# One decoder kernel, one edit: local attention's normalising roots shared and its background work kept in program order, media attention kept in program order with its routing spread wider

## The chip, the core and the metric

The kernel runs on one core of a Trainium2 chip. The metric is device time in microseconds (us), the median of three runs. Durations and waits below come from one profiled execution, whose own time stands in the table further down.

## What is computed

Two layers of a pre-norm decoder over x of shape 8 x 512 x 256 (float32). Cut to what matters here:

```python
x = x + self_attention(layernorm(x))
x = x + cross_attention(layernorm(x), ctx, ctx, adj, mask)     # 16 heads of 16
x = x + local_transformer(layernorm(x))                        # two layers l = 0, 1 of:
    #   h = shift_token(x); q, k, v = split(h @ wqkv[l])       # 8 heads of 64
    #   q, k = l2norm(q) * qs, l2norm(k) * ks; q, k = rotary_xpos(q, k)
    #   o = windowed softmax(q k^T) v                          # window 128, own and previous block
    #   x = x + o @ wo[l];  x = x + gated_gelu_ffn(norm(shift_token(x)))
x = x + quantized_attention(layernorm(x))
x = x + media_attention(layernorm(x), ctx, key_mask)           # 8 heads of 64
x = x + switch_moe(layernorm(x))                               # 8 experts, capacity 512, top 1
```

The edit touches the two local attentions, the media attention and the part of the mixture of experts (the routing) that runs beside the media attention.

## The kernel before

The 4096 rows lie in SBUF as `self.x`, 32 tiles of 128 rows; one batch row b is four of them. Stages follow one another in `fast_stages`, and each stage prepares the first batch row of the next one while it finishes (`Ahead.step`). The order on an engine is not the order of the Python code: the framework's list scheduler places an instruction when its inputs and buffers look ready to it, lower-numbered work first. Two tools of the code overrule it. `high_priority(AT_ONCE)` lets a block go ahead of whatever else is ready. `issue_after(ins)` puts what the block traces on the engine of `ins` behind `ins` in that engine's queue; it is an order only, not a wait. `together` (line 1461) uses both to keep the 4, 8 or 16 matmuls of one score or weighting group adjacent. In the cross attention, `paced` holds prepared vector work behind the softmax multiplies of the iteration before the last one.

`local_attention` (line 1832 on) is used for both layers. Its main loop goes over pairs of steps. A step pair computes the scores of one of four head pairs c of one batch row (`scores`: 8 matmul tiles, then the mask added by VectorE at L2003, then the exponential by ScalarE at L2007), then the weighted values of the head pair before (`weigh`, L2014 and L2031) and, for every second c, the row sums. These form the backbone. Between them the loop issues background work, a few small closures ("thunks") at a time:

- `prepare(b + 1)`: transposes of the rows (`turn`, L1869), twelve projections (`project(b, i, j)` for row tile i and j = q, k, v, L1885), the rotary step (`rotate`) and the transposes of q and k by heads (`turn_heads`, L1928, evacuated by ScalarE at L1931). A q or k projection leaves PSUM twice on ScalarE: as its square (L1892) and as a copy (L1893). A v projection leaves on VectorE (L1890). `rotate` runs wholly on VectorE as soon as both q and k of one row tile exist: sum of squares (L1901), a 128x16 reciprocal root by Newton steps (L1905, L1473 to L1477: eleven small instructions), and five passes over q and k (L1908 to L1919).
- `later`, a heap of delayed thunks (`Background`). Its clock advances by one per `tick`. The softmax sums go to DRAM and back (`inverted`), are multiplied in on GpSimd (`times_rows`), and the output projection `project_out` follows (L2057), whose result VectorE adds to the rows at L2062. The four projections of a batch row are entered 4 ticks after the division.

Projections, transposes and output projections share two PSUM banks named `pj`; in the cross attention there is one. So whoever evacuates a `pj` bank decides when TensorE may write it again.

`stage_media_attention` (line 2813 on) is built alike: `scores` and `weigh` are the backbone, `prepare(b + 1)` and `later` the background, two ticks' worth of thunks at most per step. After the last output projection of a batch row, `route(b)` enters the routing: statistics, normalisation (L157), two transposes (L3065), the router matmuls (L3074), choice of the expert, counting (L3105, L3106), placement, and four indirect DMAs from GpSimd (L3137) that send the rows to their slots.

Of the kernel before, what the change touches and what calls it, by code (L numbers as in the profile page):

```python
# [1277 lines left out]
class FastDecoder(Decoder):  # L1278
# [553 lines left out]
    def local_attention(self, l, y, ahead):  # L1832
# [45 lines left out]
        def project(b, i, j):  # L1878
            d = held[b]
            if j == 0:  # L1880
                d["qk"] = self.alloc(first, [P, 2 * S], F32, "la_qk", bufs=3)
                d["sq"] = self.alloc(first, [P, 2 * S], F32, "la_sq")
# [6 lines left out]
            if j == 2:  # L1889
                nc.vector.tensor_copy(d["v"][:, i, :], ps)  # L1890
# [6 lines left out]
        def rotate(d, i):  # L1897
            qk = d["qk"]
            ss = self.alloc(first, [P, 16], F32, "la_ss")
            rn = self.alloc(first, [P, 16], F32, "la_rn")  # L1900
# [11 lines left out]
            r = self.alloc(first, [P, 2 * S], F32, "la_r")  # L1912
# [7 lines left out]
            d["rows", i] = qk  # L1920
# [15 lines left out]
        def prepare(b):  # L1936

            def P_(i, j):
                return lambda: project(b, i, j)

            def T_(i):
                return lambda: turn_heads(b, i)
# [20 lines left out]
        with self.tc.tile_pool(  # L1963
# [21 lines left out]
            def scores(n):  # L1985
# [33 lines left out]
            def weigh(n):  # L2019
# [24 lines left out]
                def divide(rows):  # L2044
# [9 lines left out]
            def project_out(b, i):  # L2054
# [7 lines left out]
                nc.vector.tensor_tensor(yt, yt, ps[:, :C], ALU.add)  # L2062
# [3 lines left out]
            for pair in range(0, n + 2, 2):  # L2066
# [751 lines left out]
    def stage_media_attention(self, w, out):  # L2818
# [5 lines left out]
        with self.tc.tile_pool(reuse_waits="tile", name="ma", bufs=2) as pool, self.tc.tile_pool(  # L2824
# [153 lines left out]
            for pair in range(0, n + 2, 2):  # L2978
# [37 lines left out]
    def routing(self, pool, psum, later, out):  # L3016
# [18 lines left out]
        def route(b):  # L3035
# [483 lines left out]
```

## Time and profile before

| | us |
|---|---|
| median of 3 runs (lowest, highest) | 3094.61 (3087.45, 3096.63) |
| the profiled execution | 3094.66 |
| its span, first to last instruction | 3092.7 |
| TensorE busy in the span | 2842.4 (92%) |
| VectorE / ScalarE / GpSimd busy | 2158.3 / 1155.1 / 409.6 |
| mean granted TensorE clock | 0.974 |

The stages lie one after another in the span: cross attention up to about 662 us, with the start of local attention 0 woven into its end; local attention 0 to about 1120; its feed-forward part to about 1400; local attention 1 to about 1810; its feed-forward part to about 2080; quantized attention to about 2390; media attention to about 2840; experts to the end. Cut into such stretches, TensorE is busy as follows (each row of the table is from a table of stretches of 80 us; the columns are busy us of 80).

| stretch (us) | TensorE | VectorE | ScalarE | granted clock |
|---|---|---|---|---|
| 480 to 560, cross attention | 76.36 | 76.09 | 59.62 | 1.00 |
| 560 to 640, cross into local attention | 62.90 | 74.25 | 47.74 | 0.94 |
| 640 to 720, cross into local attention | 59.62 | 57.13 | 27.13 | 0.94 |
| 880 to 960, local attention 0 | 74.19 | 66.49 | 30.57 | 0.98 |
| 1520 to 1600, local attention 1 | 74.64 | 65.92 | 31.93 | 1.00 |
| 2560 to 2640, media attention | 77.56 | 52.80 | 30.49 | 1.00 |

"Busy" is the time in which an engine had an instruction in work, and "granted clock" is the share of full speed that TensorE was allowed. In the list of waits each line names an instruction group, what released it, the sum of the idle time before it in us, how often, and the longest.

### The profile page before, as it was taken

The page shows a single profiled execution, that of the slowest core. Times are in us where ns is not written, and L with a number is a line of the kernel's source. Part 1 is how long each engine was busy: PE and PEld are TensorE (multiplying, and loading weights), DVE is VectorE, ACT ScalarE, POOL GpSimd, SP SyncE. Part 2 cuts the span into 40 slices and gives each one's busy share as a digit, 9 for nine tenths or more (in the row PEclk, how much of TensorE's full clock was granted, in tenths as well). Part 3 has the DMA queues.
Part 4 walks back from the last instruction along what each step waited for, and adds up shares of the span by engine and source line. Part 5 has one row for each costly group of instructions (what it writes and reads, how often), then busy time and mean ns, then how long its engine had stood idle before and what let it go on. Part 6 is the DMA issues. An engine that isn't in the chain of part 4 may idle for free. (4 is left out here: it accounts for less than half of the span.)

```text
span 3092.7 us, 40203 instructions
## 1 busy us (share of the span) xinstructions
PE 2842.4 (92%) x14929; PEld 1507.6 (49%) x14944; DVE 2158.3 (70%) x4962; ACT 1155.1 (37%) x1623; POOL 409.6 (13%) x389
## 2 busy tenths in 40 slices
PE   8999999969999999999999999999786999997998
PEld 5653333225555556555555556555344334434665
DVE  7458999977887894357887898548788766665110
ACT  2237777724334321124344331115263443441111
POOL 1111111100001010000101111112111123231111
PEclk9999999989999999999999999999997999998999
DMA  7011212101001001001000012010332122223231
GB/s 242 1 35 50 71 49 70 36 19 56 15 15 29 15 24 36 0 1 43 22 15 22 22 38 69 14 41 28 125 122 76 52 93 83 90 69 96 98 139 61
DMA packets 130696, 168.74 MB, mean 55 GB/s; under 512 B 51760, under 2 KB 79665, under 8 KB 128442
## 3 DMA queue, kind: packets, MB, share of 16 engines
q1 hardware_dynamic: 126394, 154.48, 16.0%
q0 software_dynamic: 4096, 11.59, 1.0%
q8 instruction: 119, 1.95, 0.3%
q14 instruction: 87, 0.71, 0.1%
HBM read 113.12 MB, written 47.50 MB: 52 GB/s over the span
## 5 line engine op out<-in xcount | busy, mean ns | idle before, releaser
L1885 PE MATMUL pj<-w,la_hT 128*128 128x512 f32 x720 | 342.8, 615 | 32.7 <-DVE x L2062 16.3
L1732 DVE TENSOR_TENSOR x_e<-x_e,x_share 128x1024 f32<-128x1024 f32 x256 | 317.6, 1283 | 16.7 <-ACT x_e L1731 16.5
L1731 ACT ACTIVATE x_e<-sc 128x1024 f32<-128x1024 f32 x256 | 249.4, 1023 | 82.0 <-PE sc L1720 82.0
L1885 PEld LDWEIGHTS pj<-w,la_hT 128*128 128x128 f32 x720 | 131.7, 194 | 189.3 <-issue 118.1
L2007 ACT ACTIVATE la_e<-la_e 128x1024 f32<-128x1024 f32 (+1 forms) x128 | 121.1, 952 | 209.2 <-DVE la_e L2003 209.2
L2890 ACT ACTIVATE ma_e<-sc,ma_bias 128x1024 f32<-128x1024 f32 x128 | 135.8, 1110 | 165.3 <-PE sc L2884 165.3
L2216 ACT ACTIVATE lf_gate<-pj,lf_b 128x512 f32<-128x512 f32 (+1 forms) x82 | 56.3, 687 | 346.6 <-PE pj L2195 337.2
L2897 DVE TENSOR_TENSOR ma_esum<-ma_esum,ma_e 128x1024 f32<-128x1024 f32 x96 | 129.8, 1353 | 71.3 <-ACT ma_e L2890 34.8
L2195 PE MATMUL pj<-lf_hnT,w 128*128 128x512 f32 (+1 forms) x368 | 171.7, 595 | 0.6 <-DVE lf_hid L2221 0.6
L2003 DVE TENSOR_TENSOR la_e<-sc,la_mask 128x1024 f32<-128x1024 f32 (+1 forms) x128 | 137.0, 1081 | 41.1 <-PE sc L1995 41.0
L3262 POOL TENSOR_TENSOR la_oT<-la_o,x_wide 128x512 f32<-128x512 f32 x64 | 88.3, 1387 | 571.0 <-DMA x_wide<-invs 315.4
L1748 PE MATMUL po<-x_e,x_v 128*32 128x512 f32 x1024 | 138.1, 612 | 21.9 <-DVE x_e L1732 15.2
L2195 PE MATMUL sc<-lf_hnT,w 128*128 128x512 f32 x336 | 157.9, 592 | 0.0
L1720 PE MATMUL sc<-x_q,x_k 32*128 32x512 f32 x1024 | 151.3, 640 | 1.7 <-DVE sa_ok L1448 1.4
L2267 PE MATMUL po<-w,lf_hid 128*128 128x256 f32 x640 | 148.8, 379 | 0.0
L2221 DVE SCALAR_TENSOR_TENSOR lf_hid<-sc,lf_b,lf_gate 128x512 f32<-128x512 f32 x70 | 52.4, 748 | 126.9 <-PE sc L2195 126.9
L1995 PE MATMUL sc<-la_qkT 64*128 64x256 f32 (+1 forms) x1024 | 124.2, 373 | 12.3 <-ACT la_qkT L1931 11.3
L1892 ACT ACTIVATE la_sq<-pj 128x512 f32<-128x512 f32 x120 | 71.4, 595 | 170.3 <-PE pj L1885 170.3
L2057 PE MATMUL pj<-w,la_oT 128*128 128x256 f32 x512 | 122.3, 385 | 11.3 <-DVE x L2062 9.4
L2884 PE MATMUL sc<-ma_qT,ma_kT 64*128 64x512 f32 x512 | 129.9, 626 | 0.0
L2267 PEld LDWEIGHTS po<-w,lf_hid 128*128 128x128 f32 x640 | 117.8, 190 | 20.2 <-issue 6.7
L2908 PE MATMUL po<-ma_e,ma_v 128*64 128x512 f32 x512 | 124.2, 606 | 0.0
(493 smaller groups left out, 5296.2 us busy)
## 6 DMA issues: line engine op xcount, KB each, us to landing
x_wide<-invs SPq DMA_DIRECT2D x184, 128.0 KB
w<-in_f_w_dram SPq DMA_DIRECT2D x16, 1024.0 KB
kv<-kv_o SPq DMA_DIRECT2D x56, 256.0 KB
slots<-x_empty SPq DMA_DIRECT2D x8, 1028.0 KB
x_mask<-in_x_maskT_dram SPq DMA_DIRECT2D x8, 1024.0 KB
ma_kT<-kv SPq DMA_DIRECT2D x8, 1024.0 KB
ma_v<-kv SPq DMA_DIRECT2D x8, 1024.0 KB
ex_rows<-slots SPq DMA_DIRECT2D x7, 1028.0 KB
```

The costliest lines, as they stand in the source:

```text
L1720: nc.tensor.matmul(pair[r // 2][:, r % 2, :], d["k"][rows, g, kt * P : (kt + 1) * P], d["q"][rows, e, g, :], start=True, stop=True,)
L1731: nc.scalar.activation(ex, d["e"][rest][p], AF.Exp)
L1732: nc.vector.tensor_tensor(ex, ex, d["share"][:, kt, :].unsqueeze(1).broadcast_to([P, 2, 512]), ALU.mult)
L1748: nc.tensor.matmul(d["po"][32 * r : 32 * r + 32, :], d["v"][:, kt, 8 * g + 2 * r + e, :], ex[r // 2][:, r % 2, :], start=(kt == 0), stop=( ...
L1885: nc.tensor.matmul(ps, d["hT"][:, k, i * P : (i + 1) * P], wqkv[:, k, j * S : (j + 1) * S], start=(k == 0), stop=(k == 1),)
L1995: nc.tensor.matmul(both[half][:, r, jj * 256 : jj * 256 + to - j * P], d["qkT"][rows, 4 + c, j * P : (j + 1) * P], d["qkT"][rows, c, j * P ...
L2003: nc.vector.tensor_tensor(ex[:, :, :n_cols], ps[:, :, :n_cols], mask[:, :n_cols].unsqueeze(1).broadcast_to([P, 2, n_cols]), ALU.add,)
L2195: nc.tensor.matmul(ps[:m, :], w1[:, k, at : at + m], held[b]["hnT"][:, k, :], start=(k == 0), stop=(k == 1))
L2267: nc.tensor.matmul(ps[:, :C], held[b]["hid"][:, f, i * P : (i + 1) * P], w2[:, f, :], start=(f == 0), stop=False,)
L2884: nc.tensor.matmul(both[m // 2][:, r, :], d["k"][rows, c, kt * P : (kt + 1) * P], d["q"][rows, c, :], start=True, stop=True,)
L2890: nc.scalar.activation(ex, ps, AF.Exp, bias=bias[:, b * NST + kt : b * NST + kt + 1], scale=0.125)
L2897: nc.vector.tensor_tensor(d["sum", c], d["sum", c], ex, ALU.add)
```

## The change

In local attention:

- `in_turn()` is new. It queues the TensorE instructions of its block behind the newest TensorE instruction traced so far. Every background thunk and every tick of the main loop now runs inside it, and the stepping of the next stage at the end of the loop too. Backbone instructions are not bound by it.
- `rotate` is cut into `square` (the sum of squares of one row tile), `root` (one reciprocal root for two row tiles, 128x32) and `rotate` (the five passes). `prepare` lists them in a new order: two q/k tiles are projected, squared and rooted before the first is rotated, and all v projections come last, each beside a `turn_heads`. The number of thunks is 18 before and after.
- The v projection leaves PSUM on ScalarE and no longer on VectorE.
- `la_qk` has 4 buffers where it had 3; `la_r` has 1 where it had 2.
- The mask addition and the addition of the output projection get the priority `AT_ONCE` on VectorE.
- The output projections are entered 9, 12, 15 and 18 ticks after the division, where all four were entered at 4.

In media attention, background thunks and ticks run inside `in_turn()`; and for batch rows 0 to 5 the routing's delays grow by 2 ticks up to the choice of the expert and by 4 from the counting on.

```diff
+    def in_turn(self):
+        return self.tc.issue_after(self.newest(mybir.EngineType.PE))
...
             if j == 0:
-                d["qk"] = self.alloc(first, [P, 2 * S], F32, "la_qk", bufs=3)
+                d["rows", i] = self.alloc(first, [P, 2 * S], F32, "la_qk", bufs=4)
...
             if j == 2:
-                nc.vector.tensor_copy(d["v"][:, i, :], ps)
+                nc.scalar.copy(d["v"][:, i, :], ps)
             else:
                 nc.scalar.activation(d["sq"][:, j * S : (j + 1) * S], ps, AF.Square)
-                nc.scalar.copy(d["qk"][:, j * S : (j + 1) * S], ps)
+                nc.scalar.copy(d["rows", i][:, j * S : (j + 1) * S], ps)
             if j == 1:
-                rotate(d, i)
+                d["sq", i] = d["sq"]
+
+        def square(b, i):
+            d = held[b]
+            if i % 2 == 0:
+                d["ss"] = self.alloc(first, [P, 2, 16], F32, "la_ss")
             nc.vector.tensor_reduce(
-                ss, d["sq"].rearrange("p (h d) -> p h d", d=64), AX.X, ALU.add
+                d["ss"][:, i % 2, :], d["sq", i].rearrange("p (h d) -> p h d", d=64), AX.X, ALU.add
             )
+        def root(b):
+            d = held[b]
+            d["rn"] = self.alloc(first, [P, 2, 16], F32, "la_rn")
+            ss, rn = (x.rearrange("p i h -> p (i h)") for x in (d["ss"], d["rn"]))
             nc.vector.tensor_scalar(ss, ss, 1e-24, None, ALU.max)
             self.rsqrt(first, rn, ss, "la_rt")
+        def rotate(b, i):
+            d = held[b]
+            qk, rn = d["rows", i], d["rn"][:, i % 2, :]
...
-            r = self.alloc(first, [P, 2 * S], F32, "la_r")
+            r = self.alloc(first, [P, 2 * S], F32, "la_r", bufs=1)
...
             return [
-                [lambda: turn(b, 0), lambda: turn(b, 1), P_(0, 0)],
-                [P_(0, 1), P_(1, 0)],
-                [P_(1, 1), P_(0, 2)],
-                [P_(2, 0), T_(0)],
-                [P_(2, 1), P_(1, 2)],
-                [P_(3, 0), P_(3, 1), T_(1)],
-                [P_(2, 2), T_(2)],
-                [P_(3, 2), T_(3)],
+                [one((turn, 0)), one((turn, 1)), one((p, 0, 0)), one((p, 0, 1), (s, 0))],
+                [one((p, 1, 0)), one((p, 1, 1), (s, 1), (root,))],
+                [one((p, 2, 0), (r, 0)), one((p, 2, 1))],
+                [one((p, 3, 0), (r, 1)), one((p, 3, 1))],
+                [one((p, 0, 2), (s, 2)), one((t, 0), (s, 3), (root,))],
+                [one((p, 1, 2), (r, 2)), one((t, 1))],
+                [one((p, 2, 2), (r, 3)), one((t, 2))],
+                [one((p, 3, 2)), one((t, 3))],
             ]
...
-                    nc.vector.tensor_tensor(
-                        ex[:, :, :n_cols], ps[:, :, :n_cols],
-                        mask[:, :n_cols].unsqueeze(1).broadcast_to([P, 2, n_cols]), ALU.add,
-                    )
+                    with self.tc.high_priority(self.AT_ONCE):
+                        nc.vector.tensor_tensor(
...
-                            later.add(4, lambda i=i: project_out(b, i))
+                            later.add(9 + 3 * i, lambda i=i: project_out(b, i))
...
-                nc.vector.tensor_tensor(yt, yt, ps[:, :C], ALU.add)
+                with self.tc.high_priority(self.AT_ONCE):
+                    nc.vector.tensor_tensor(yt, yt, ps[:, :C], ALU.add)
...
                 for i in (pair, pair + 1):
-                    later.tick(1)
+                    with self.in_turn():
+                        later.tick(1)
                     if i < n:
                         for thunk in ready[i % 8]:
-                            thunk()
-                            later.tick(1)
+                            with self.in_turn():
+                                thunk()
+                                later.tick(1)
                     if i == n - 6:
                         early.close()
                     if i > n - 6:
-                        ahead.step()
+                        with self.in_turn():
+                            ahead.step()
...
                         if thunk is not None:
-                            thunk()
-                    later.tick(2)
+                            with self.in_turn():
+                                thunk()
+                    with self.in_turn():
+                        later.tick(2)
...
+            slow = 2 if b < B - 2 else 0
             later.add(1, stats)
             later.add(2, norm)
-            later.add(3, lambda: turn(0))
-            later.add(4, lambda: turn(1))
-            later.add(5, logits)
-            later.add(6, choose)
-            later.add(8, count)
-            later.add(9, place)
+            later.add(3 + slow, lambda: turn(0))
+            later.add(4 + slow, lambda: turn(1))
+            later.add(5 + slow, logits)
+            later.add(6 + slow, choose)
+            later.add(8 + 2 * slow, count)
+            later.add(9 + 2 * slow, place)
             for i in range(NST):
-                later.add(10 + i, lambda i=i: send(i))
+                later.add(10 + 2 * slow + i, lambda i=i: send(i))
```

More of the change, by code (lines that the diff above doesn't have):

```diff
@@ L1889, in project @@
             if j == 2:
-                nc.vector.tensor_copy(d["v"][:, i, :], ps)
+                nc.scalar.copy(d["v"][:, i, :], ps)
             else:
                 nc.scalar.activation(d["sq"][:, j * S : (j + 1) * S], ps, AF.Square)
-                nc.scalar.copy(d["qk"][:, j * S : (j + 1) * S], ps)
+                nc.scalar.copy(d["rows", i][:, j * S : (j + 1) * S], ps)
             if j == 1:
-                rotate(d, i)
[L1897 to L1900, printed above, removed]
+                d["sq", i] = d["sq"]
[3 more added lines that the diff above has]
+                d["ss"] = self.alloc(first, [P, 2, 16], F32, "la_ss")
             nc.vector.tensor_reduce(
-                ss, d["sq"].rearrange("p (h d) -> p h d", d=64), AX.X, ALU.add
+                d["ss"][:, i % 2, :], d["sq", i].rearrange("p (h d) -> p h d", d=64), AX.X, ALU.add
             )
+        def root(b):
+            d = held[b]
+            d["rn"] = self.alloc(first, [P, 2, 16], F32, "la_rn")
+            ss, rn = (x.rearrange("p i h -> p (i h)") for x in (d["ss"], d["rn"]))
             nc.vector.tensor_scalar(ss, ss, 1e-24, None, ALU.max)
             self.rsqrt(first, rn, ss, "la_rt")
+        def rotate(b, i):
+            d = held[b]
+            qk, rn = d["rows", i], d["rn"][:, i % 2, :]
             q3 = qk.rearrange("p (h d) -> p h d", d=64)
@@ L1919, in rotate @@
             nc.vector.tensor_tensor(qk, qk, r, ALU.add)
-            d["rows", i] = qk
         def turn_heads(b, i):
@@ L1936, in prepare, with one, thunk @@
         def prepare(b):
[L1938 to L1942, printed above, removed]
-            return [
-                [lambda: turn(b, 0), lambda: turn(b, 1), P_(0, 0)],
-                [P_(0, 1), P_(1, 0)],
-                [P_(1, 1), P_(0, 2)],
-                [P_(2, 0), T_(0)],
-                [P_(2, 1), P_(1, 2)],
-                [P_(3, 0), P_(3, 1), T_(1)],
-                [P_(2, 2), T_(2)],
-                [P_(3, 2), T_(3)],
+            def one(*calls):
+                def thunk():
+                    for f, *args in calls:
+                        f(b, *args)
+                return thunk
+            p, t, s, r = project, turn_heads, square, rotate
+            return [
+                [one((turn, 0)), one((turn, 1)), one((p, 0, 0)), one((p, 0, 1), (s, 0))],
[6 more added lines that the diff above has]
+                [one((p, 3, 2)), one((t, 3))],
             ]
@@ L2002, in scores @@
                     ex = self.alloc(pool, [P, 2, 512], F32, "la_e", bufs=6)
-                    nc.vector.tensor_tensor(
-                        ex[:, :, :n_cols], ps[:, :, :n_cols],
-                        mask[:, :n_cols].unsqueeze(1).broadcast_to([P, 2, n_cols]), ALU.add,
-                    )
+                    with self.tc.high_priority(self.AT_ONCE):
+                        nc.vector.tensor_tensor(
+                            ex[:, :, :n_cols], ps[:, :, :n_cols],
+                            mask[:, :n_cols].unsqueeze(1).broadcast_to([P, 2, n_cols]), ALU.add,
+                        )
                     nc.scalar.activation(ex[:, :, :n_cols], ex[:, :, :n_cols], AF.Exp, scale=-1.0)
```

## The prediction

> **What bounds the kernel.** I read the page's first part, then a table of stretches, then TensorE's list of waits in each stretch, and last the timelines of the worst places. TensorE is busy for 2842.4 of 3092.7 us, and where it is the bound, only its idle time and its lost clock can be won.
>
> [...] By the rows the change has no part in that: it removes or adds no matmul[...]. So I let only the idle time count, and nothing below it.
>
> Three stretches inside the stages that are touched, from the table of stretches (columns: stretch; its length; busy us and instructions of TensorE, weight loads, VectorE, ScalarE, GpSimd; granted clock; DMA share; GB/s):
>
> ```profile
> 720.00:1110.00 390.00, 363.11 (x2177) 208.38 (x2177) 317.43 (x632) 158.26 (x256) 38.02 (x39) 0.99 0.07 20
> 1360.00:1790.00 430.00, 402.21 (x2247) 231.33 (x2246) 334.29 (x639) 171.76 (x280) 39.25 (x38) 1.00 0.07 22
> 2390.00:2800.00 410.00, 389.86 (x1668) 164.60 (x1666) 282.60 (x688) 167.42 (x188) 104.12 (x95) 0.99 0.22 73
> ```
>
> TensorE idles 27, 28 and 20 us in them, so they hold 75 us at most. The waits of TensorE in the first stretch (local attention 0; sum, times, longest):
>
> ```profile
> PE pj L1885 <- DVE x L2062: 8.2, 12, 0.9
> PE sc L1995 <- ACT la_qkT L1931: 5.7, 6, 0.9
> PE pj L2057 <- DVE x L2062: 4.7, 6, 0.8
> PE pj L1928 <- DVE la_rn L1473: 4.3, 7, 1.0
> PE pj L1928 <- DVE la_qk L1919: 1.4, 4, 0.8
> ```
>
> Half of it is a `pj` bank that waits for VectorE to add an output projection; the waits come in every batch row and none is over 1 us. Layer 1 shows the same lines with 8.1, 5.6, 4.7, 3.8 and 1.3. In media attention one line carries it:
>
> ```profile
> PE pj L3065 <- DVE mo_rows L157: 12.9, 6, 2.4
> ```
>
> The dearest place is the seam between cross attention and local attention 0, 560 to 720 us, where TensorE idles 17.1 + 20.4 = 37.5 us. Its timeline and stretches:
>
> ```profile
> 635.36 3.78 PE L1885 MATMUL pj<-w,la_hT 128*128 128x512 f32 x4 [10.13 <-DVE la_v L1890]
> 658.73 3.78 PE L1885 MATMUL pj<-w,la_hT 128*128 128x512 f32 x4 [4.18 <-DVE la_v L1890]
> 663.98 1.98 PE L1885 MATMUL pj<-w,la_hT 128*128 128x512 f32 x4
> ...
> 630.00:635.40 5.40, 0.04 (x1) 0.04 (x1) 5.13 (x11) 0.00 (x0) 0.00 (x0) 0.50 0.00 0
> 635.40:639.20 3.80, 3.80 (x8) 1.26 (x12) 3.80 (x4) 0.00 (x0) 0.00 (x0) 0.50 0.00 0
> ...
> 596.00:662.00 66.00, 47.94 (x244) 14.46 (x244) 59.99 (x100) 32.53 (x43) 3.47 (x2) 0.88 0.08 17
> ```
>
> With a single `pj` bank here, a v projection waits for a copy that stands on VectorE behind a whole rotation. But VectorE works through the stall (5.13 of 5.40), and from 596 to 662 it is busy 60 of 66 us: this seam is bound by VectorE, and freeing the bank alone does not free it.
>
> **The seam, step by step.** The change takes from VectorE, for batch row 0: four v copies (684 ns each, L1890), 2.7 us; and two of four root chains. One chain in the timeline runs from 628.78 to 631.04, 2.26 us; eleven instructions of some 0.17 us do not get twice as long for 32 columns instead of 16[...] (I allow 0.2 us), so 2 x 2.1 = 4.2. Together 6.9 us less on the bounding engine. The copies go to ScalarE (580 ns each at L1893), which is idle half of this stretch; what is queued behind them there are exponentials, up to 0.6 us later.
>
> Then the clock. [...]after 10.13 and after 4.18 us a projection took 3.78 instead of 1.98 us, so each costs 1.8 more. [...]by the rows a 2.16 us wait in media attention is followed by 4.7 us at a clock of 0.67 (1.55 lost, after one of six such gaps), and three stretches of 10 us in local attention 0 (800, 910, 1030 us) stand at 0.83, 1.7 us each, with no gap over 1 us near. [...]by the rows up to 3.6 + 1.5 + 5.1. I take 3 at the seam, 4 in the local attentions and 1 in media, since the rows decide.
>
> Seam: 6.9 + 3 = 10 us gained. Bounds: 0 (the last output projections arrive through a chain of DMAs, a wait for `x_wide` that ends only at 679.5, whatever VectorE does) and 25 (two thirds of the 37.5).
>
> **The local attentions, both layers' loops.** (a) Output projections: 12.9 + 12.8 = 25.7 us of waits. They are entered three ticks apart instead of in a burst, and their addition (0.41 us) goes ahead on VectorE; it still waits for an instruction in work, at most 1.4 us, while the other bank covers a projection. I leave 4: gain 22. (b) Transposes waiting for rotations (L1473, L1919, and L1893): 6.2 + 6.6 = 12.8. A rotation now stands two groups ahead of its `turn_heads`, some 14 us against its five passes of 5.2 (rows L1908 to L1919): gain 8. (c) Scores waiting for the last `la_qkT` copy, 5.7 + 5.6: `turn_heads(3)` is still the last thunk of a row, nothing gained. (d) The clock, 4.
>
> (e) What the order costs. A projection takes 1.78 us (18 records in 7.99 us in one unbroken run, four records each) and is evacuated in 1.17 by ScalarE, so runs of projections are safe with two banks. A `turn_heads` is not: each half is 0.55 us of TensorE and 0.58 of ScalarE copy plus some 0.1 of signalling. Walked through with two banks (v projection, half, half, v projection), 0.16 + 0.06 us stay exposed; with 56 of them in the two loops, 12 us. Before, backbone matmuls were placed between the halves and hid this. After `turn`, the first projection waits for `la_hT`, 0.43 where it shows (14 times: 6). I take 12 of these 18, since the next scores are not bound by the order and can fill some; bounds 0 and 36 (then all of (a), (b) and (d) is given back). 22 + 8 + 4 - 12 = 22 us gained.
>
> What lies beside other work: 56 v copies in the loops (14 batch rows of four) cost ScalarE 56 x 0.58 = 32 us over two stages where it is busy 158 of 390 and 172 of 430 us; VectorE loses 14 x 6.9 = 97 us over both loops, where it stood at 317 of 390, and that gives nothing directly. `la_r` with one buffer only orders VectorE against itself. `la_qk` with four covers the four tiles now held until their transposes. If the ScalarE cover were gone, each projection would wait for its bank; that is the rival below. No DMA is moved in this part.
>
> **Media attention.** Six waits, batch rows 0 to 5, are exactly those whose transposes are moved by 2 ticks (some 7 us); the chain they wait for (statistics, eleven root instructions, four normalisations) was late by 2.2 us. All 12.9 go. The program order forbids early transposes of `prepare`, which have shown one 2.0 us wait; the routing's transposes and logits now meet them in the same ticks on two banks: I charge 2. Counting, placing and the 24 indirect DMAs (1179 ns each on GpSimd's queue) move by 4 ticks; queued behind them are `ma_oT` multiplications and copies into `ma_esum`, on a GpSimd busy 104 of 410 us, and nobody reads the slots before the experts. Batch rows 6 and 7 keep their delays, so the end (11.8 us for the first expert's rows) stays. With 1 of clock: 12 gained; bounds 8 and 15.
>
> **Sum.** 10 + 22 + 12 = 44 us. The profiled execution took 3094.66 and the median is 3094.61, so they need no correction: 3050.6.
>
> **Rivals.**
> - *The order gives back what it wins in the local attentions*: (e) at its bound of 36, gain 0 there; the seam gives 8 and media 12: 3075. For it: every wait of the loops is under 1 us and small enough to be only renamed, and TensorE's order was already filled densely. Against: the largest line is removed by priority and spacing, not by order.
> - *More goes*: (a), (b) and (d) in full with the gaps of (e) filled by backbone work, 45; the seam 25, media 14: 3011. For it: VectorE falls from 81% to about 70% of the loops, so its queue shortens for everything.
> - *Slower: ScalarE's queue takes over the `pj` banks.* ScalarE now evacuates all projections and all transposes, in TensorE's strict order. If each half of a `turn_heads` meets one exponential (1.06 us) ahead of its copy, 112 halves lose 119 us, of which 12 are charged already: 3158. It decides from 44 / 112 = 0.4 us per half on. Against: two exponentials per 14 us of loop, ScalarE under half busy.
> - *It does less than it says*: the order binds background TensorE work alone; if the scheduler had it so already, seam and media come partly and the rest cancels: about 3090, within the noise, if media's waits are renamed too.
>
> **How the numbers follow.** Forecast (3030 to 3062) 0.45, given back 0.19, more 0.20, slower 0.10, no change 0.06 (it does less). Predicted time 3051. The range reaches to the two neighbours that gain, 3011 and 3075, with media and seam at their ends (sizes of both signs in (e)): 3008 to 3084. A measurement of this kernel can tell 0.3% (9 us) from no change: faster 0.84, within 0.06, slower 0.10.
>
> **What would show it.** In the new profile: the waits on the added output projection (L2062's successor) under 3 us per layer, or (a) is wrong; waits of transposes on `la_qkT` and `la_v` copies by ScalarE of about 12 us in all, or (e) is; no 10 us gap and at most one half-clock stretch in the seam, with VectorE busy there about 7 us less; no `mo_rows` wait before batch row 6; half as many root instructions (192 become 96). The prediction is wrong if TensorE's idle time over the two loops does not fall from 55 us to some 36, or if the idle time stays and busy time falls.

## The result, and the profile after

The changed kernel takes 3051.07 us (median of four runs, 3046.02 to 3056.84), the kernel before beside it 3091.31 us. The ratio is 0.9865 with a 95% interval of [0.9846, 0.9883]. By the ratio that is 41.7 us less (the medians differ by 40.2), where the sum had 44. The profiled execution took 3056.84 us, the slowest of the four, with a span of 3054.9 (before: 3092.7), so the profile shows 37.8 of it.

To see where the time came from I read in both traces when certain instructions first start (before / after, the line numbers of the new kernel are a few higher):

| first start of | before | after | stretch that ends here, change |
|---|---|---|---|
| scores of local attention 0 | 696.0 | 696.9 | seam and all ahead of it: +0.9 |
| second product of feed-forward 0 | 1159.2 | 1145.9 | local attention 0: -14.2 |
| scores of local attention 1 | 1401.6 | 1387.5 | feed-forward 0: -0.8 |
| second product of feed-forward 1 | 1855.0 | 1831.9 | local attention 1: -9.0 |
| scores of media attention | 2391.5 | 2367.0 | feed-forward 1 and quantized: -1.4 |
| first expert product | 2851.9 | 2814.0 | media attention: -13.4 |

The seam gave nothing where 10 had been forecast, the two local attentions 23.2 (22), the media attention 13.4 (12). How much such differences mean can be read from later kernels that run the same instructions in a stage. Four profiles of the same local attentions (the kernel after and three below, without one of the orders or the media part) lie at 448.9 to 450.6 us and 442.5 to 444.4. Ten profiles of the same seam put the first scores anywhere from 687.9 to 700.7 us, so for the seam one profile says little. The same stretches as before, moved to where they now lie, from the table of stretches of the kernel after (columns: stretch; its length; busy us and instructions of TensorE, weight loads, VectorE, ScalarE, GpSimd; granted clock; DMA share; GB/s):

```profile
708.00:1098.00 390.00, 367.04 (x2243) 214.95 (x2241) 293.21 (x500) 181.46 (x294) 44.23 (x40) 1.00 0.07 21
1388.00:1818.00 430.00, 403.98 (x2400) 232.90 (x2397) 322.47 (x679) 193.89 (x313) 47.97 (x43) 0.99 0.10 29
2365.00:2775.00 410.00, 399.28 (x1723) 167.52 (x1723) 294.25 (x718) 173.37 (x196) 112.17 (x98) 1.00 0.22 75
```

VectorE has less to do, ScalarE more, as the diff says. TensorE's idle time in the media stretch fell from 20 to 11 us; in the local ones it is still 23 and 26. TensorE's waits in local attention 0 of the kernel after (sum, times, longest):

```profile
PE pj L1939 <- DVE x L2076: 16.2, 16, 1.6
PE po L2027 <- ACT la_o L2044: 3.4, 2, 3.1
PE pj L1939 <- ACT la_qkT L1942: 2.8, 1, 2.8
...
PE pj L1889 <- ACT la_qkT L1942: 1.6, 1, 1.6
```

The wait on the added output projection, which was to fall to under 3 us a layer, rose from 12.9 to 16.2 (layer 1: 12.8 to 14.5). It only changed its victim: a projection or an output projection before, a transposition of the heads now. The waits on the rotation are gone but for 0.4 us, and so are those of the scores on `la_qkT`, which I had left standing. This is one such wait in the timeline, first TensorE, then VectorE (start, duration, engine, line; in brackets the idle time before it and what ended it):

```profile
831.61 1.99 PE L2070 MATMUL pj<-w,la_oT 128*128 128x256 f32 x8
833.44 1.88 PE L1889 MATMUL pj<-w,la_hT 128*128 128x512 f32 x4
836.90 0.66 PE L1939 MATMUL pj<-ident,la_qk 128*128 128x128 f32 x4 [1.58 <-DVE x L2076]
```

```profile
833.49 0.69 DVE L1928 TENSOR_TENSOR la_r<-la_qk,la_sin 128x512 f32<-128x512 f32 x1
834.10 0.68 DVE L1929 TENSOR_TENSOR la_r<-la_qk,la_sin 128x512 f32<-128x512 f32 x1
834.70 0.68 DVE L2055 COPY la_total<-sum 128x512 f32<-128x512 f32 x1
835.30 1.21 DVE L1930 TENSOR_TENSOR la_qk<-la_qk,la_cos 128x1024 f32<-128x1024 f32 x1
836.44 0.41 DVE L2076 TENSOR_TENSOR x<-x,pj 128x256 f32<-128x256 f32 x1
```

The output projection is done at 833.6. Its addition has priority, but that only chose its place when the queue was laid down; behind the instruction in work three more still stand ahead of it, and it starts 2.8 us later. A row of the table of stretches says why:

```profile
822.00:852.00 30.00, 26.68 (x165) 16.34 (x163) 29.36 (x48) 12.39 (x21) 1.77 (x1) 1.00 0.07 19
```

In these 30 us of a batch row's 56, VectorE is busy for 29.36. Over the whole row it is busy 40 of 56, and that average is what I had argued from. In the 30 us that matter there is no slack. The kernel before had such a half too (here with 28.31 us):

```profile
826.00:856.00 30.00, 27.71 (x138) 16.89 (x136) 28.31 (x50) 9.60 (x16) 2.95 (x2) 1.00 0.06 19
```

The additions do come sooner than before. Counted over the timelines of local attention 0, they start on average 1.6 us behind their projection, where it was 2.5 us. But now only a v projection of 1.9 us stands between the projection and a transposition that takes the same bank.

### The profile page after: what moved, and what is told of

Read it like the earlier page. It is cut to its first block, busy times and chain, and to the rows that moved or that the text cites. A ratio compares the mean times of both kernels' runs of the same rounds, so it can differ in the third digit from the quotient of the medians.

```text
span 3054.9 us, 39805 instructions
## 1 busy us (share of the span) xinstructions
PE 2839.3 (93%) x14929; PEld 1513.9 (50%) x14944; DVE 2063.4 (68%) x4546; ACT 1192.1 (39%) x1687; POOL 428.7 (14%) x389
## 5 line engine op out<-in xcount | busy, mean ns | idle before, releaser
L1889 PE MATMUL pj<-w,la_hT 128*128 128x512 f32 x720 | 333.3, 603 | 5.2 <-ACT la_qkT L1942 4.5
L1736 DVE TENSOR_TENSOR x_e<-x_e,x_share 128x1024 f32<-128x1024 f32 x256 | 315.8, 1276 | 14.3 <-ACT x_e L1735 14.2
L3283 POOL TENSOR_TENSOR la_oT<-la_o,x_wide 128x512 f32<-128x512 f32 x64 | 97.9, 1541 | 753.0 <-DMA x_wide<-invs 647.9
L2914 DVE TENSOR_TENSOR ma_esum<-ma_esum,ma_e 128x1024 f32<-128x1024 f32 x96 | 120.6, 1260 | 58.8 <-ACT ma_e L2907 30.0
L2027 PE MATMUL po<-la_e,la_v 128*64 128x256 f32 (+1 forms) x1024 | 125.2, 369 | 6.7 <-ACT la_o L2044 6.0
```

The source lines that it names most:

```text
L1736: nc.vector.tensor_tensor(ex, ex, d["share"][:, kt, :].unsqueeze(1).broadcast_to([P, 2, 512]), ALU.mult)
L1889: nc.tensor.matmul(ps, d["hT"][:, k, i * P : (i + 1) * P], wqkv[:, k, j * S : (j + 1) * S], start=(k == 0), stop=(k == 1),)
L2027: nc.tensor.matmul(out[:, j * P : to], lhsT(j), ex[:, jj * 256 : jj * 256 + to - j * P], start=(j == 0), stop=(j == 3), skip_group_check=True,
```

## Experiments

Two lines of thought stand against each other in them. That of the forecast: the gain comes from order, spacing and priority, and the relief of VectorE acts in the seam alone. Its rival: the order does nothing, and the gain in the local attentions comes from the VectorE work that was taken away. Each expectation puts them into numbers for its kernel. The ratios are to the kernel before on the same chip, which took 3091.3 to 3098.0 us; the kernel after stands at 0.9865.

### Is the order in the local attention worth anything?

```diff
-                    with self.in_turn():
-                        later.tick(1)
+                    later.tick(1)
```

(likewise at the other two places of the loop)

> The changed kernel without the program order in local attention (the three uses of in_turn in its loop are taken out; the new list of prepared work, the shared roots, the v copies on ScalarE, the priorities and the spacing stay). Theory A: the order itself removed the small stalls of the transposes and the scores, so taking it out brings back some 10 to 20 us (about 3062 to 3071, with 3051 for the changed kernel). Theory B: the built program issues TensorE's work of both loops in the same order with and without it, all but one transpose at the end of layer 1, so nothing moves: within 5 us of the changed kernel, ratio to before 0.985 to 0.988, and the waits of the loops the same to 2 us.

3055.8 us, 0.9859 [0.982, 0.9899], and the same waits on the added projection, 16.4 and 14.6. In the two traces TensorE's sequences differ in the place of one transposition, at the end of local attention 1, and those of VectorE and ScalarE not at all. The order binds nothing here (theory B). This run also serves as the kernel after on this chip.

### What is the media part worth?

```diff
-            slow = 2 if b < B - 2 else 0
+            slow = 0
...
-                            with self.in_turn():
-                                thunk()
+                            thunk()
```

> The changed kernel with the media attention and the routing delays of before. From the traces the stretch from the first media scores to the first expert matmul fell by 13.4 us (460.4 to 447.0). Theory: parts add up, so this one loses 12 to 14 us: about 3064, ratio to before 0.990 to 0.992, and six waits of the routing's transposes on mo_rows of some 2.1 us are back. Rival: part of the fall was a better clock by chance, then it loses 8 or less.

3065.5 us, 0.9906 [0.9875, 0.9938]; the media stretch takes 460.5 us again, as before the change (447.0 after). The wait on the routing's rows in TensorE's list of waits, first here, then in the kernel after:

```profile
PE pj L3082 <- DVE mo_rows L157: 17.3, 8, 3.9
```

```profile
PE pj L3084 <- DVE mo_rows L157: 2.0, 1, 2.0
```

That is the wait of the forecast, and its size (over the same stretch the kernel before has 17.1 us, with the waits of the last two batch rows). Later I took away the order alone and kept the delays:

```diff
-                    with self.in_turn():
-                        later.tick(2)
+                    later.tick(2)
```

> The kernel after, with the wider routing delays of the media attention but without its issue in program order. Theory A (the order in the media attention carries part of the 13.4 us that the media stretch gave): the stretch from the first media scores to the first expert product goes from 447.0 us back to some 453, and the whole to some 3057. Theory B (the order does nothing, because TensorE's instructions were already issued in nearly that order; the wider delays carry all of it): the stretch stays at 447 to 450 us and the whole at 3051 to 3056 (0.986 to 0.987 of before).

0.9867 [0.9843, 0.9891], and a media stretch of 449.9 us. The wider delays carry the media part. The order adds 3 us at most, and more likely nothing: the kernel without the order in local attention, which keeps the media order, has 449.6 us as well. Over all kernels with the wider delays the stretch is 447.0 to 450.7 us, so they are worth 10 to 13 us.

### Is it VectorE's work?

Each of the two reliefs was undone alone. First the v copies:

```diff
-                nc.scalar.copy(d["v"][:, i, :], ps)
+                nc.vector.tensor_copy(d["v"][:, i, :], ps)
```

> The changed kernel with the v projections of local attention copied out of PSUM by VectorE, as before, all else as changed. Theory A: VectorE is not the bound in the loops (51 to 64 busy of 80 us), so this costs only the seam, 2 to 4 us: ratio to before 0.986 to 0.988. Theory B: in the new list every v projection stands right before a transpose on the same two banks, and VectorE serves its queue late (the added output projection waited 1.0 us each time), so 64 more bank releases wait for it: 56 in the loops at 0.5 to 1 us, 20 to 50 us slower, with waits of L1939 on la_v by DVE of that size.

3078.17 us, 0.9944 [0.9924, 0.9964]: of the gain of 1.35% only 0.56% is left. Local attention 0 takes 456.6 us instead of 449.0, local attention 1 453.9 instead of 444.4, of which 6.5 and 8.1 us are idle time of TensorE; the waits are spread over copies of turned heads (9.1 us), the added projection (12.6) and the rotation (2.7; these three in local attention 0). The time is that of theory B, but its wait is not: TensorE waits on VectorE's `la_v` copies for 0.4 us in each attention. Then the roots:

```diff
-                [one((p, 1, 0)), one((p, 1, 1), (s, 1), (root,))],
+                [one((p, 1, 0)), one((p, 1, 1), (s, 1), (root, 1))],
...
-            ss, rn = (x.rearrange("p i h -> p (i h)") for x in (d["ss"], d["rn"]))
+            ss, rn = d["ss"][:, i % 2, :], d["rn"][:, i % 2, :]
```

(a root of its own for each of the four row tiles, 128x16 each, right after its squares)

> The changed kernel with one reciprocal root per row tile (128x16) right behind its squares, in the new order of the list; VectorE works 32 chains of 2.26 us (72 us) more than with the shared roots, 56 of 64 row tiles lie in the loops. Theory A: VectorE is under its bound there, so the shared root is worth at most the seam: within 5 us of the changed kernel (ratio 0.985 to 0.988). Theory B: VectorE's lateness makes the waits of TensorE in the loops, and the extra chains in front of the mask additions and the added output projections bring 10 to 25 us.

3087.11 us, 0.9972 [0.996, 0.9984]. Nearly the whole gain is lost, more than either theory had, although the media stretch keeps its part (449.9 us). The profiled execution is one of the fastest of its 21 runs (3081.34 us) and shows 24.5 us of the loss, 18.7 of them in the two attentions (454.7 and 457.4 us). What that looks like in local attention 1, and in the full stretch of a batch row of local attention 0:

```profile
PE pj L1940 <- DVE x L2077: 19.6, 7, 3.6
```

```profile
820.00:850.00 30.00, 27.84 (x159) 16.61 (x159) 29.45 (x69) 13.42 (x23) 3.96 (x2) 0.94 0.06 17
```

VectorE is as full there as in the kernel after, with more to get through. The same wait is now rarer and up to 3.6 us long, and TensorE's clock falls: 0.97 over local attention 1, where it was 0.99. Of the 13.0 us that this attention lost, 5.0 are idle time and 8.0 are TensorE at work for longer. So, by the ratios, shared roots (69 us of VectorE's time in all, from the rows of the five root instructions that write `la_rt`, `la_rn` and `la_ss`, 140.6 against 71.2; one of their Newton instructions took 198 to 205 ns on 128x16 here and 191 to 192 on 128x32 in the kernel after) were worth 33 us while the v copies stay on ScalarE, and the v copies (64 of 0.68, 44 us) 24 us while the roots stay shared. Each is about half of what it takes from VectorE. The two don't add: with one of them undone the attentions keep only 4.5 (roots) and 6.1 us (copies) of their gain, with both in place it is 23.2, a fifth of the 113 us. Both edits also shift the order of VectorE's queue, so amount and place of its work are not told apart here, and the new list was not run alone.

### Priority, spacing, and the bank

```diff
-                    with self.tc.high_priority(self.AT_ONCE):
+                    with nullcontext():
```

(for the mask add and the output add)

> The changed kernel without the priority AT_ONCE on the mask addition and on the addition of the output projection in local attention. The changed kernel still waits 16.2 + 14.5 us for the added output projection, so the priority does not do what the prediction had it do. Theory A: it still holds those waits down, and without it they grow by 5 to 15 us per layer (3061 to 3081). Theory B: VectorE's queue is served in an order fixed beforehand and has room, so the priority is worth within 5 us.

3063.85 us, 0.9889 [0.9845, 0.9933]: by the ratios 7 us slower than the kernel after, but the intervals overlap, so no effect is shown. The waits on the added projection did not grow, as theory A had it, but fell to 8.5 and 11.3 us, and others of 3 to 5 us on copies of turned heads came up. Next the spacing:

```diff
-                            later.add(9 + 3 * i, lambda i=i: project_out(b, i))
+                            later.add(4, lambda i=i: project_out(b, i))
```

> The changed kernel with the output projections of local attention entered together, 4 ticks after the division, as before. Theory A: the spacing put each output projection right before a v projection and a transpose that needs its bank, and so keeps 30 us of waits; entering them together costs nothing or even gains, within 5 us, waits on the added projection of 20 to 35 us in both layers. Theory B: the spacing is what pays, and the burst brings the loops back to the period of before (58.6 us a batch row against 56.0), 20 to 35 us slower: 3071 to 3086.

3044.01 us, 0.983 [0.979, 0.987]: faster than the kernel after by some 7 to 12 us. This interval alone still reaches into that of the kernel after; a kernel further down that runs the very same instructions ([0.9802, 0.9842]) does not. In the profiles the two attentions gain 9.9 us (444.8 and 438.8); the seam starts its scores 7.5 us earlier, which is another matter (below). The output projections of one row, TensorE's timeline:

```profile
812.82 1.89 PE L2070 MATMUL pj<-w,la_oT 128*128 128x256 f32 x8
...
817.59 3.72 PE L2070 MATMUL pj<-w,la_oT 128*128 128x256 f32 x16 [1.17 <-DVE x L2076]
...
822.87 1.89 PE L2070 MATMUL pj<-w,la_oT 128*128 128x256 f32 x8
```

They stand near one another ahead of the next row's transpositions, with q and k projections between them, and one waits 1.17 us. In the kernel after, the spacing puts them at 831.6, 839.7, 847.1 and 853.9, each just ahead of a v projection and a transposition that needs its bank: 1.58, 1.04 and 0.70 us lost. It is not that VectorE has room where the burst lies: from 810 to 826 us it is busy for 15.43 of 16. But the additions start 0.7 us behind their projection on average (1.6 in the kernel after), and no transposition presses behind them. Waits on the added projection fall to 3.8 and 3.5 us a layer, which is what I had expected of the spacing. I also gave the output projection another bank, that of the row sums:

```diff
-                ps = self.pj()
+                ps = self.pj() if b == B - 1 else self.alloc(psum, [P, 512], F32, "sum")
```

> The changed kernel with the output projections of local attention (all batch rows but the last) written to the PSUM bank of the row sums and no longer to the two pj banks. Theory A: the waits of the transposes on the added output projection (16.2 + 14.5 us) are a wait for a pj bank, so they go, and the row sums' bank is free most of the time: 15 to 28 us faster (ratio 0.977 to 0.982). Theory B: the wait moves to the next output projection or to the row sums, which now wait for VectorE themselves: within 6 us.

3056.37 us, 0.9873 [0.9854, 0.9893]: nothing (theory B). The waits in local attention 0:

```profile
PE sum L2070 <- DVE la_total L2055: 9.6, 6, 2.1
PE sum L2070 <- DVE x L2076: 4.5, 10, 1.4
```

The wait follows into the other bank, since it is the same VectorE queue that has to empty it.

### The seam

```diff
-                    nc.vector.tensor_tensor(
+                    with self.tc.high_priority(self.AT_ONCE) if b == B - 1 else nullcontext():
+                        nc.vector.tensor_tensor(
```

(the softmax multiply of the cross attention's last batch row)

> The changed kernel with the softmax multiplies of the cross attention's last batch row (VectorE) given the priority AT_ONCE, so that rotations of local attention 0 no longer stand before them; in the changed kernel TensorE waits 7.65 + 2.8 + 2.7 + 1.6 us for them at the seam. Theory A: the seam is bound by VectorE's total work and by the chain of DMAs behind the last weighting; multiplies first end the cross attention 6 to 10 us earlier, that chain starts earlier and the rotations fill the time of the chain: 5 to 10 us faster (ratio 0.982 to 0.985). Theory B: the rotations then come late and the first scores of local attention wait for them: within 3 us.

3060.8 us, 0.9887 [0.9868, 0.9906]: no gain; the seam's wait on that multiply is 14.4 us instead of 16.8. That wait is new in this size. Before and after, from TensorE's list of waits from 540 to 720 us:

```profile
PE po L1748 <- DVE x_e L1732: 5.6, 6, 1.8
PE po L1752 <- DVE x_e L1736: 16.8, 8, 7.6
```

So where 14.3 us of waits on `la_v` went, 11.2 came up at another instruction that waits for VectorE. What else held the seam is seen when the kernel after is laid beside the one with projections together: the last output projections of the cross attention, first after, then together.

```profile
676.74 2.07 PE L1785 MATMUL pj<-w,x_oT 128*128 128x256 f32 x4 [0.68 <-ACT la_qkT L1942]
679.32 2.07 PE L1785 MATMUL pj<-w,x_oT 128*128 128x256 f32 x4 [0.51 <-DVE x L1790]
```

```profile
675.89 1.13 PE L1785 MATMUL pj<-w,x_oT 128*128 128x256 f32 x4 [0.67 <-ACT la_qkT L1942]
677.54 1.13 PE L1785 MATMUL pj<-w,x_oT 128*128 128x256 f32 x4 [0.51 <-DVE x L1790]
```

Eight of them follow one another, at half clock in one kernel (0.52 granted from 676 to 697 us) and at full in the other (1.00): 8 x 0.94 = 7.5 us. The first local scores then start at 696.9 and 689.4, a difference of the same 7.5 us. (The second kernel also begins the groups 0.85 us earlier and has two longer gaps, of 0.93 and 1.01 us; these cancel.) The edits are not what sets the clock, since both kernels run the same instructions in the same order up to this point; the last section comes back to it.

### How far it goes

With everything taken back that had shown no use (order, priority, spacing), so that shared roots with their new list, the v copies on ScalarE and the wider media delays are left:

> The kernel after with four of its edits taken back at once: no program order anywhere, no priority on the mask add and the output add, the output projections entered together as before. Left are the new list with shared roots, the v copies on ScalarE and the wider media delays. Theory A (priority is worth the 8 us that the run without it alone suggests, the spacing costs 12): some 3050 us, 0.9865 of before. Theory B (priority was only of use against the late adds that the spacing made; the three parts that are left carry everything): 3042 to 3046, like the kernel with projections together, 0.984.

3045.67 us, 0.9832 [0.9813, 0.9851], like the kernel with projections together (theory B). The kernel without the media order alone, on the same chip, took 3060.86. Then two attempts at more, both from the kernel with projections together. The copy of v at once:

```diff
+                with self.tc.high_priority(self.AT_ONCE):
+                    nc.scalar.copy(d["v"][:, i, :], ps)
```

> Output projections entered together, and the copy of v put ahead of other work on ScalarE. In the kernel with projections together TensorE still waits 7.6 us in each local attention for the copy of v before a transposition. Theory A (that copy stands behind work of ScalarE that nobody waits for): most of 15 us goes, some 3031 us, 0.980 of before. Theory B (ScalarE has nothing to spare there and the copy is at once in any case, or it pushes copies of the turned heads back): no gain within 3 us, 3041 to 3047.

3041.12 us, 0.9822 [0.9802, 0.9842]; the waits of 7.6 us in each attention stay to the digit. The traces say why: on TensorE, VectorE and ScalarE the instructions are the same in the same order as without this priority. So it changed nothing, and the run serves as a second measurement of the kernel with projections together. And the copy of the row sums to ScalarE:

```diff
-                nc.vector.tensor_copy(total, ps)
+                nc.scalar.copy(total, ps)
```

> Output projections entered together, and the copy of the row sums (0.69 us, two for each batch row, 32 in all, so 22 us of VectorE's work) given to ScalarE. Theory A (VectorE is full for some 30 of a row's 56 us, and work taken from it there comes out as time at a half to all of its size): 8 to 20 us off the kernel with projections together, some 3024 to 3036 us, 0.978 to 0.981 of before. Theory B (VectorE costs nothing beyond the waits named in the trace; with projections together only 3.8 and 3.5 us of waits on VectorE are left): 0 to 7 us off, or slower by ScalarE's added work, 3037 to 3050.

3064.61 us, 0.9894 [0.9876, 0.9913]: 20 us slower than with projections together, outside what either theory had, though VectorE has 22 us less to do. In the profiles the two attentions lose 4.9 and 10.9 us of it. Transpositions now wait 17.5 and 16.9 us for copies of turned heads. One of them, ScalarE and TensorE:

```profile
843.24 1.06 ACT L2020 ACTIVATE la_e<-la_e 128x1024 f32<-128x1024 f32 x1 [4.06 <-DVE la_e L2016]
844.20 0.57 ACT L1942 COPY la_qkT<-pj 128x512 f32<-128x512 f32 x1
```

```profile
844.82 0.66 PE L1939 MATMUL pj<-ident,la_qk 128*128 128x128 f32 x4 [2.29 <-ACT la_qkT L1942]
```

ScalarE is not short of time: it stands idle for 4.06 us, waiting for a masked score from VectorE, and the copy that TensorE needs is queued behind that. The same copy in the kernel with projections together stands ahead of the same exponentials:

```profile
836.20 0.59 ACT L1942 COPY la_qkT<-pj 128x512 f32<-128x512 f32 x1 [1.67 <-PE pj L1939]
839.06 1.79 ACT L2020 ACTIVATE la_e<-la_e 128x1024 f32<-128x1024 f32 x2 [2.28 <-DVE la_e L2016]
```

On TensorE this place in the queue cost 2.29 us. That is the mechanism of the slower rival (copies behind an exponential), set off by moving two copies per batch row; why the scheduler then laid the queue down in the other order, the traces do not say. So half an us gained per us taken from VectorE is what roots and v copies were each worth here; it is no rule.

## Why the prediction was right, and where its steps failed

The time was right, 3051 against 3051.07, and so were two of its three sums; several of the terms inside them were not. That it agrees to a tenth of a us is luck: the four runs lie between 3046 and 3057, the kernel before measured 3 us less beside it, and errors of over 20 us cancel inside the local sum. By its own sign (TensorE's idle time over the two loops from 55 us to some 36) the local part failed: in stretches of the same length 49 us are left, and over the two whole attentions it fell by 14.0 us, not 19.

- **Media, 12 forecast, 13.4 measured.** Right in place, cause and size: the kernel without the media part has the waits and the 13 us back. The wider delays did it; what I charged to the order (2) is not to be seen.
- **Seam, 10 forecast, nothing measured.** The waits on `la_v` (14.3 us) are gone and VectorE is busy 7 us less (124.2 of 160, 131.4 before), as forecast, but the wait on the softmax multiplies grew by 11.2 us. The other failed term is the clock, put at +3: in this profile it was about -7.5, by a half-clock stretch (from 676 to 697 us a clock of 0.52, before 0.94), and my test "at most one half-clock stretch" failed as well. Over the ten profiles of the same seam instructions the first scores start 1.3 us earlier than before on average, 8.1 us earlier in the best. Against one profile of the kernel before, no gain is shown.
- **Local attentions (a), 22 from waits on output projections.** Failed. I took spacing and priority to free the bank. The additions did start sooner, but the waits rose by 5 us, because the spacing put each projection 1.9 us ahead of a transposition that takes its bank, while VectorE is full and the addition waits its turn. Entered together they fell nearly as I had written (3.8 and 3.5 us left).
- **(b) 8 from rotations that stand earlier.** They went, all but 0.4 us of 12.8, and more: the waits of the scores on `la_qkT` (c), put at no gain, went too, 11.3 us. (In the kernel with everything taken back those are there again, 15.0 us, and it is faster all the same.)
- **(e) the cost of the order, 12.** The order does nothing, so it costs nothing. There are waits on ScalarE's copies, some 8 us over both loops (2.8 and 1.6 in the list above, 2.2 and 1.6 in layer 1), but each is a single wait and not the 56 small ones that I had walked through.
- **"That gives nothing directly", of VectorE's 97 us in the loops.** This is the wrong step that made up for (a). I took 317 busy of 390 us to mean slack. The runs with a relief undone lost 24 and 33 us: here work taken from an engine that is full for 30 of 56 us showed up as time, directly and through the clock (in attention 1 a clock of 0.97 and 0.98 with a relief undone, 0.99 with both).
- **Below the busy time nothing can be won.** Assumed, and not so here: TensorE's busy time fell by 9.2 us in the two attentions (6.2 and 3.0), idle time by 14.0. In attention 0 the clock accounts for two fifths: the traces have 15.4 us at half clock there before and 10.6 after, 2.4 us. For the rest, and for the 3.0 in attention 1, where half clock rose from 3.4 to 6.8 us, no run gives a cause; that stays open.

Of the rivals, "it does less than it says" named the true mechanism of the order, but not what else was in the change. The slower one did not happen in this change.

## What to carry to other kernels

Ask for an engine's busy share in the stretch where others wait for it, not over the stage: 72% of a row was 98% of the half that counts here, and of three trials that moved VectorE's work, two changed the time by about half of it (the third went the other way). Before an ordering or a priority is given credit, compare the instruction sequences with and without it; twice here they were the same, but for one transposition. Look at what stands behind delayed work: spread out, each projection stood right ahead of an instruction that needed its bank, and that cost 10 us in the two attentions against a burst. A copy moved to an idle engine still stands in that engine's queue, behind whatever that queue is waiting for: here ScalarE stood idle for 4.06 us ahead of such a copy, and TensorE lost 2.29.

## What was not expected of the hardware

In the kernel after TensorE stayed at half clock for some 21 us with gaps of 0.51 to 0.56 us only, busy for 80% of the time (stretch; length, TensorE's busy time, clock, DMA share, GB/s):

```profile
676.00:697.00 21.00, 16.69 (x35) 0.52 0.07 26
```

Among the profiles of the kernel after and the twelve experiments, ten show a clock of 0.50 to 0.61 in this stretch and three (projections together, everything taken back, roots apart) 1.00. In all of them the clock also falls for 3 to 10 us at a time earlier in the seam, about its longer waits (0.74 to 0.83 over 640 to 660 us).

The spell is not made by an edit. Ten of these kernels (all but those with the v copies on VectorE, the roots apart or the softmax multiplies first) run the same instructions in the same order on TensorE, VectorE and ScalarE until after the seam, and two of the ten were at full clock. Projections together and its twin with the priority on the copy of v are the same throughout; one has full clock here (1.00), the other 0.54.

The traces' record of the granted clock shows what differs. In the traces of the kernels before and after, the half-clock stretches (24 and 20) start whole steps of 3.41 us apart and last one to eight of them (the last is cut off by the end). The steps lie differently against the work: in the kernel after one begins with the first of the eight groups (676.76 and 676.74 us), with projections together 0.81 us ahead of it (675.08 and 675.89). All ten spells are 23.9 us long, seven steps. The step before the spell and its first step in the kernel after, then a step at the same place with projections together:

```profile
673.35:676.76 3.41, 1.38 (x10) 1.00 0.12 39
676.76:680.18 3.42, 2.91 (x6) 0.50 0.00 0
```

```profile
671.66:675.08 3.42, 2.07 (x11) 1.00 0.15 41
```

The light stretch of transpositions ahead of the eight groups fell into one step there (1.38 of 3.41 us busy), and was shared between two here (2.07 us in each). With projections together no step from the earlier half-clock spell to the first scores is under 55%, and with everything taken back no stretch of 5 us from 660 to 685 us is under 59%. In the spell of the kernel after the clock stayed at half through steps of 72 to 85%, and was full again behind the first step without a gap (697.24 us on). This is what these traces show and not a limit that was measured: in the kernel before, one step with 1.72 of 3.41 us busy (at 670.4 us) passed without a fall.

With projections together the eight groups have the same gaps of 0.51 to 0.56 us, and two of 0.93 and 1.01 besides, at full clock (1.00). So gaps of this size are not enough by themselves.
